# Score tiles of two head pairs in one row, sums over keys in place, and the products of a graph in a new order

## The chip, the cores and the metric

The kernel runs on one core of one Trainium2 chip. The metric is the device time in microseconds (us), lower being better. The engines that work here are TensorE (PE in the profile, its weight loads PEld), VectorE (DVE), ScalarE (ACT) and SyncE (SP), which issues all DMAs. GpSimd is idle.

## The reference

Two graph layers are applied one after the other to 32 graphs of 512 nodes with 512 features each, in float32. The first is attention with 8 heads of 64, weighted by the adjacency, with a residual and a layer norm; the second is a graph attention whose logits are a sum of two scalars per node pair. Cut to what matters:

```python
# layer 0
q, k, v = x @ Wq.T + bq, x @ Wk.T + bk, x @ Wv.T + bv      # per head: 512 x 64
logits  = q @ k.T / sqrt(64) + log(clip(adj, 1e-8))        # per head: 512 x 512
x1      = layer_norm(x + softmax(logits) @ v @ Wo.T + bo)
# layer 1
f       = x1 @ fc_w.T + fc_b
masked  = leaky((f @ q_w + q_b) + (f @ k_w + k_b).T + (1 - adj) * -1e9)
out     = softmax(masked) @ f + x1
```

## The kernel before

**Tiling.** A graph's matrices lie in SBUF as four chunks of 128 partitions. Heads are worked in pairs: two heads of 64 fill 128 partitions, so a graph has four *slots*, p = 0 to 3 (`slot(b, p)`, L1278). The attention is kept transposed, keys on partitions: for each of four key chunks kc, `score` (L838) multiplies kT by qT for both heads (two matmuls of 64 rows each, 512 columns, into two PSUM banks), and ScalarE writes exp of it into a tile `at` of 128x2x512 (L858; L856 where the tile is *halved*, that is, where its two halves lie in two single banks). `factors` (L861) multiplies by the clipped adjacency `cT` (L866), which gives the same weights as adding its logarithm before the exponential. `values` (L881, matmul L891) multiplies v by `at`, two heads side by side in columns of 64. `sums` (L871) adds the four `at` of a pair into a tile `as` (L876, L879), and `divide` (L902, matmul L908) sums `as` over the partitions with a matrix of ones, 32 columns at a time. The sums go to DRAM and back (`d0`, `c`), are inverted in `divided` (L922) and come back spread over all partitions as `R`, with which `scale` (L942) multiplies the values' results `oT`.

**Products in seven parts.** The products q and k (`seven_qk`, L624), v (`seven_v`), with Wo (`seven_wo`), Z = softmax x (`seven_z`, L1001) and the last with fc_w (`seven_out`, L779) are done on 2x2 blocks with seven half-size products each instead of eight, by additions on VectorE between them. They all go through `halves` (L210): 128 rows, 64 columns, two matmuls side by side. In `seven_z`, `before0`, `before1`, `after0`, `after1`, `before2`, `after2` and `after3` are these additions; product 6 needs what `after0` writes.

**PSUM.** The pool ps_s has two tiles of two banks each, which scores and the q/k products use in turn; ps_o has one bank for the values; `lone` is a list of three single banks mx, my, mz for the other products, for `divide` (the first of them) and for halved score tiles (the other two).

**Stages.** Three graphs are in work at once. While graph b is in its four slots, graph b-1 gets Wo, the norm and its layer 1 logits, and graph b-2 gets Z and the output. The weights of layer 1 of graph b-1 are made by `softmax` (L1117), a list of units from `weigh_units` (L424): logits of chunks 0 and 1, of 2 and 3, then `weights` (leaky on VectorE and exp on ScalarE by turns, L446 and L447), then `blocks`, which spreads the result e into the tile `eP` by 16 DMAs of 64 KB (L148). `eT` (L1074) transposes eP in blocks of 32 on VectorE (L572); Z of the graph cannot start before. The three users of the io pool's one buffer (x of the next graph, the work tile w, and eP) take turns.

**Order.** The order on TensorE, VectorE, ScalarE and SP is the order in which the program calls the operations; no planner changes it, and each engine takes its own list from front to back. In a slot the order is: first half of the last pair's values, score tiles 0 and 1, factors of them, score tiles 2 (halved) and 3, `divide` in slots 0 and 2, second half of the values, and then a product of that slot: Z in slot 0, Wo in slot 1, the output in slot 2 (`layer1_rows`, L1418), v of the next graph in slot 3. The q/k products of the next pair are laid between. The tag `at` has 6 buffers and `as` 2.

Of the kernel before, what the change touches and what calls it, by code (L numbers as in the profile page):

```python
# [19 lines left out]
P = 128  # L20
# [10 lines left out]
def kernel(  # L31
# [392 lines left out]
    def weigh_units(s, small, work, name):  # L424


        e = s["e"]
        s["r"] = small.tile([P, NC], FP, tag="r", name=f"r_{name}")
        top = small.tile([P, NC], FP, tag="top", name=f"top_{name}", bufs=2)
        nm = small.tile([P, NC], FP, tag="nm", name=f"nm_{name}", bufs=2)  # L430

        def logits(cs):
            for c in cs:
                qk = work[c % len(work)]
                nc.scalar.activation(qk, s["kb"], AF.Identity, bias=s["q"][:, c : c + 1])  # L435
# [27 lines left out]
    def scaled(s, cs):  # L463
        nc.vector.tensor_mul(s["yb"][:, cs, :], s["n"][:, cs, :], over(K["gamma"], cs))
# [39 lines left out]
    def fast(ctx):  # L504
# [333 lines left out]
        def score(b, p, kc, apart=False):  # L838

            s = S[b]  # L840
            halved = kc == 2 and not apart
            if halved:
                parts = lone[1:]
            else:
                sc = ps_s.tile([P, 2, N], FP, tag="s", name=f"sc_{b}_{p}_{kc}")
                parts = [sc[:, j, :] for j in range(2)]
            for j in range(2):
                rows = slice(j * DK, (j + 1) * DK)
                nc.tensor.matmul(  # L849
                    parts[j], s["kT", p][rows, ts(kc, P)], s["qT", p][rows, :],  # L850
                    start=True, stop=True,
                )
            at = act.tile([P, 2, N], FP, tag="at", name=f"at_{b}_{p}_{kc}", bufs=6)
            if halved:
                for j in range(2):
                    nc.scalar.activation(at[:, j, :], parts[j], AF.Exp, scale=SCALE)  # L856
            else:
                nc.scalar.activation(at, sc, AF.Exp, scale=SCALE)  # L858
            s["at", p, kc] = at
# [103 lines left out]
        def divide_here(b, p):  # L963

            s = S[b]
            ps = ps_s.tile([P, 2, N], FP, tag="s", name=f"ps_{b}_{p}")[:, 0, :]
            i = 2 * B - 1 + p % 2
            R = act.tile([P, 2, N], FP, tag="at", name=f"t_{b}_{p}", bufs=6)  # L970
# [146 lines left out]
        def softmax(b):  # L1117
            s = S[b]
            units = weigh_units(
                s, small, [s["w"][:, i, :] for i in ((2, 3, 0) if b == B - 1 else (2, 3))], b  # L1120
            )

            def blocks():
                s["eP"] = io.tile([P, NC, N], FP, tag="x", name=f"eP_{b}")
                spread_blocks(s["eP"], s["e"])
            return units + ([blocks] if b < B - 2 else [])

        def new_yb(b):
            S[b]["yb"] = act.tile([P, NC, D], FP, tag="yb", name=f"yb_{b}")

        def last_layer1(b):
# [5 lines left out]
            S[b]["yb"] = yb = K["qk_s"].rearrange("p a b f -> p (a b) f")[:, :NC, :]  # L1137
            places = []
            for i in range(6):
                t = act.tile([P, 2, N], FP, tag="at", name=f"l1_{i}", bufs=6)  # L1140
# [133 lines left out]
        def run(units):  # L1274
            for u in units:
                u()

        def slot(b, p):  # L1278
# [14 lines left out]
                wos[0]("a")  # L1293
            run(vals[:1])
            for kc in (0, 1):
                score(b, p, kc)
            if first:
                run(first_v[1:2])
            if p == 0 and last >= 0:
# [15 lines left out]
                if last >= 0:  # L1315
                    mask(S[last])
            for kc in (2, 3):
                score(b, p, kc, first)
            if p == 0 and last >= 0:
                divide(last, 2)  # L1320
            if p == 2 and b != 1:
                divide(b, 0)
            run(vals[1:])
            if p == 1 and last >= 0:
# [1 line left out]
            soft = softmax(last) if p == 3 and last >= 0 else []  # L1326
            run(soft[:1])
            if p == 0 and last >= 0:
                if b >= 2:
                    new_yb(b - 2)  # L1330
                    scaled(S[b - 2], slice(0, KH))
                    zs, extra = seven_z(b - 2)
                    extra[0]()
                    run(eT(b - 2))
                if b == 1:
                    turn_a((2, 3))
            if p > 0 or b < 2:
                factors(b, p, 1)
# [6 lines left out]
            if p == 0 and b >= 2:  # L1345
                extra[1]()
                run(next_qk[:4])
                zs[0]()
                extra[2]()
                run(next_qk[4:])  # L1350
                extra[3]()
                zs[1]()
                turn_a((2, 3))
                scaled(S[b - 2], slice(KH, NC))
                extra[4]()
                zs[2]()
                extra[5]()
                divided(last, 2)
                zs[3]()
                factors(b, p, 1)  # L1360
                extra[6]()
                sums(b, p, 0)
            elif p == 0:
# [54 lines left out]
        def layer1_rows(b, next_qk, norm):  # L1418
# [10 lines left out]
            run(norm[2:])  # L1429
            if b == 1:  # L1430
                run(next_qk[2:4])
                divide(b, 0)
            elif nxt == B:
                sums(b, 2, 0)
            if b >= 2 and nxt < B:
# [36 lines left out]
        def run_out(units):  # L1472
            for mul, add in units:
                mul()
                add()

        def last_slot(rest):


            b, last = B - 1, B - 2  # L1480
            for kc in (0, 1):
                score(b, 3, kc)
            run(values(b, 2))
            factors(b, 3, 0)
            sums(b, 3, 0)
# [1 line left out]
            soft = softmax(last)  # L1487
            soft[0]()
            for kc in (2, 3):
                score(b, 3, kc, True)  # L1490
            factors(b, 3, 1)
            load_e(b)
            vs = values(b, 3)
# [61 lines left out]
            outs[1][0]()  # L1555
            run(soft[:2])
            outs[2][0]()
            soft[2]()
            outs[3][0]()
            for i in range(1, 4):  # L1560
                outs[i][1]()
# [2 lines left out]
            return rest_of_layer1(find_range(), outs[4][1])  # L1564

        load_x(0)
        pair = act.tile([P, 2, N], FP, tag="at", name="first_pair", bufs=6)
        pair = [pair[:, i, :].rearrange("p (c d) -> p c d", c=DC) for i in range(2)]
        load_first_constants(pair)
        load_a(0, range(NC))  # L1570
# [167 lines left out]
```

## Time and profile before

| | |
|---|---|
| time, median of 3 runs | 3359.99 us (3356.05 to 3360.93) |
| profiled execution: its own time | 3363.72 us |
| its span, first to last instruction | 3361.9 us |
| TensorE busy, matmuls recorded | 3343.2 us (99%), 25914 |
| VectorE busy | 3004.2 us (89%), 5284 instructions |
| ScalarE busy | 1394.7 us (41%), 2501 instructions |
| DMA, share of 16 engines and mean rate | 36.2%, 75 GB/s |
| granted TensorE clock | 1.000 |

The busy table gives the time in which an engine had an instruction in work. Matmuls overlap, so a busy TensorE says little of its pace; the distance between the starts of its weight loads in the timeline says more. A timeline line has the start in us from the span's start, the time from there to the end of the group, the engine, the line of the kernel, the operation with its output and inputs, the mode and shape, how many instructions were merged (x), and in brackets the idle time ahead of it and what ended it. For a matmul, 128*64 means 128 rows by 64 columns of the array. Some matmul records are missing from a trace.

### The profile page before, as it was taken

How to read it: one execution, taken by the hardware profiler on the slowest of the kernel's cores; microseconds unless marked ns; L12 is line 12 of the kernel's file. 1: busy time of each engine (PE TensorE's matmuls, PEld its weight loads, DVE VectorE, ACT ScalarE, POOL GpSimd, SP SyncE). 2: the span in 40 equal slices, each digit the busy share in tenths (PEclk: the TensorE clock that was granted, in tenths of full speed). 3: DMA queues.
4: the chain of work that ended last, by engine and by line, in shares of the span. 5: the costliest groups of instructions: out<-in, count | busy, mean ns of one | idle time of the engine just before them, and what ended most of it. 6: DMA issues, size and time to landing. Idle time of an engine off the chain costs nothing.

```text
span 3361.9 us, 64316 instructions
## 1 busy us (share of the span) xinstructions
PE 3343.2 (99%) x25914; PEld 1886.9 (56%) x25914; DVE 3004.2 (89%) x5284; ACT 1394.7 (41%) x2501; POOL 0.9 (0%) x9
## 2 busy tenths in 40 slices
PE   9999999999999999999999999999999999999999
PEld 4555555555555555555555555555555555555555
DVE  7898989889998899898898988999889988889897
ACT  3443443434443444434444343443344443444443
POOL 0000000000000000000000000000000000000000
PEclk9999999999999999999999999999999999999999
DMA  4334333343423443333424334333344333443321
GB/s 126 50 69 92 63 87 70 58 92 79 74 71 59 88 91 62 80 67 70 92 61 88 68 61 92 68 85 67 58 92 85 68 76 65 76 91 62 84 72 45
DMA packets 881656, 252.85 MB, mean 75 GB/s; under 512 B 806732, under 2 KB 809036, under 8 KB 881352
## 3 DMA queue, kind: packets, MB, share of 16 engines
q1 hardware_dynamic: 881352, 248.67, 36.2%
q8 instruction: 206, 3.38, 0.4%
q14 instruction: 98, 0.80, 0.1%
HBM read 182.46 MB, written 34.65 MB: 65 GB/s over the span
## 4 chain that ended last, share of the span: by engine, by line
PE 94%; DVE 2%; SPq 2%; DMA 1%; ACT 1%; issue 0%; DVEq 0%; ACTq 0%
PE f L213 21%; PE my L213 15%; PE mx L213 14%; PE mz L213 14%; PE po L891 13%; PE sc L849 10%; SPq L148 1%; PE my L849 1%; PE mz L849 1%; PE mx L849 1%; DVE at L866 1%; PE my L908 1%; PE mx L908 1%; PE mz L908 1%; SPq L542 1%
## 5 line engine op out<-in xcount | busy, mean ns | idle before, releaser
L858 ACT ACTIVATE at<-sc 128x1024 f32<-128x1024 f32 x386 | 384.5, 1031 | 751.2 <-PE sc L849 751.2
L866 DVE SCALAR_TENSOR_TENSOR at<-cT,at 128x1024 f32<-128x1024 f32 x512 | 600.2, 1215 | 67.0 <-ACT at L858 67.0
L891 PE MATMUL po<-at,v 128*64 128x512 f32 x2048 | 490.0, 599 | 2.0 <-DVE fold_more L298 1.6
L849 PE MATMUL sc<-qT,kT 64*128 64x512 f32 x1544 | 387.6, 607 | 0.0
L879 DVE TENSOR_TENSOR as<-as,at 128x1024 f32<-128x1024 f32 x254 | 310.3, 1222 | 5.4
L891 PEld LDWEIGHTS po<-at,v 128*64 128x64 f32 x2048 | 135.8, 136 | 271.3 <-issue 248.6
L849 PEld LDWEIGHTS sc<-qT,kT 64*128 64x128 f32 x1544 | 138.3, 186 | 225.1 <-issue 171.9
L213 PE MATMUL f<-xT,wq 128*64 128x256 f32 x2032 | 262.6, 379 | 0.0
L213 PE MATMUL f<-T,qk_s 128*64 128x256 f32 x2032 | 251.7, 379 | 0.6 <-ACT f L651 0.6
L213 PEld LDWEIGHTS f<-xT,wq 128*64 128x64 f32 x2032 | 146.0, 137 | 100.6 <-issue 28.0
L213 PEld LDWEIGHTS f<-T,qk_s 128*64 128x64 f32 x2032 | 145.7, 137 | 74.6 <-ACT f L651 1.4
L876 DVE TENSOR_TENSOR as<-at,at 128x1024 f32<-128x1024 f32 x128 | 155.8, 1217 | 0.1
L657 ACT ACTIVATE qT<-f,bq 128x256 f32<-128x256 f32 x127 | 60.2, 474 | 229.6 <-PE f L213 229.6
L663 ACT ACTIVATE kT<-f,bk 128x256 f32<-128x256 f32 x127 | 59.8, 471 | 192.2 <-PE f L213 192.2
L213 PE MATMUL f<-xT,qk_s 128*64 128x256 f32 x1016 | 131.3, 379 | 0.0
L213 PE MATMUL f<-T,wk 128*64 128x256 f32 x1016 | 131.3, 379 | 0.0
L213 PE MATMUL f<-xT,wk 128*64 128x256 f32 x1016 | 131.3, 379 | 0.0
L213 PE MATMUL mz<-eP,n 128*64 128x256 f32 x960 | 114.3, 380 | 2.0 <-DMA c<-d 1.1
L213 PE MATMUL mx<-eP,n 128*64 128x256 f32 x960 | 114.2, 380 | 1.3 <-DVE eP L572 1.3
L213 PE MATMUL my<-eP,n 128*64 128x256 f32 x960 | 114.1, 379 | 0.5 <-DVE eP L572 0.5
L899 ACT COPY oT<-po 128x512 f32<-128x512 f32 x128 | 74.9, 585 | 71.9 <-PE po L891 71.9
L435 ACT ACTIVATE w<-w,q 128x512 f32<-128x512 f32 x128 | 85.3, 716 | 32.9 <-DVE top L436 24.9
(419 smaller groups left out, 6107.0 us busy)
## 6 DMA issues: line engine op xcount, KB each, us to landing
cT<-in_adj_dram SPq DMA_DIRECT2D x512, 64.0 KB
R<-d SPq DMA_DIRECT2D x126, 256.0 KB
x<-in_x_dram SPq DMA_DIRECT2D x124, 256.0 KB
n<-in_x_dram SPq DMA_DIRECT2D x31, 1024.0 KB
L<-in_adj_dram SPq DMA_DIRECT2D x60, 512.0 KB
eP<-L SPq DMA_DIRECT2D x480, 64.0 KB
out_dram<-yb SPq DMA_DIRECT2D x58, 512.0 KB
w<-dk SPq DMA_DIRECT2D x32, 256.0 KB
```

What stands on the lines that cost most here:

```text
L213: nc.tensor.matmul(to[ts(h, DK)], left[:, ts(h, DK)], right, start=start, stop=stop, skip_group_check=True,)
L435: nc.scalar.activation(qk, s["kb"], AF.Identity, bias=s["q"][:, c : c + 1])
L657: nc.scalar.activation(q[:, H:], ps["a"], AF.Identity, bias=bq)
L663: nc.scalar.activation(k[:, :H], ps["d"], AF.Identity, bias=bk, scale=-1.0)
L849: nc.tensor.matmul(parts[j], s["kT", p][rows, ts(kc, P)], s["qT", p][rows, :], start=True, stop=True,)
L858: nc.scalar.activation(at, sc, AF.Exp, scale=SCALE)
L866: nc.vector.scalar_tensor_tensor(at, cT[:, kc, :].unsqueeze(1).to_broadcast([P, 2, N]), ADJ_MIN, at, ALU.max, ALU.mult,)
L876: nc.vector.tensor_add(s["as", p], s["at", p, 0], s["at", p, 1])
L879: nc.vector.tensor_add(s["as", p], s["as", p], s["at", p, kc])
L891: nc.tensor.matmul(s["po", p][j * DK : (j + 1) * DK, :], s["v"][h // 4][:, kc, ts(h % 4, DK)], s["at", p, kc][:, j, :], start=(kc == 0), s ...
L899: nc.scalar.copy(s["oT"][p], s["po", p])
L908: nc.tensor.matmul(ps[h * BL : (h + 1) * BL, :], ones[:, :BL], s["as", p + h // 2][:, h % 2, :], start=True, stop=True,)
```

## The change

For graphs 2 to 30 the four slots become two halves, `first_two` (pairs 0 and 1) and `second_two` (pairs 2 and 3). Each half starts with the sum over keys of an earlier two pairs (`divide`), then makes all eight score tiles of its two pairs in a row (`eight_scores`; every third tile, counting from the first, is halved), and has all its products and both pairs' values (`both`) behind them. Between those the factors are applied one tile at a time (`factor`). The sums over keys are added into the pair's first attention tile after the values have read it (`sums_in_place`), so that no tile `as` is needed; `at` gets 8 buffers. In layer 1, leaky becomes a unit of its own, ahead of the four exponentials, and the logits use three parts of w instead of two for every graph. All 16 loads of cT for the next graph are issued together, after the last factor. The last graph's first slot becomes `joining_slot`, its other slots stay; graphs 0 and 1 keep the slots, with the part for b >= 2 taken out of `slot`.

```diff
@@ weigh_units @@
-        def weights():
+        def leaky():
             nc.vector.tensor_scalar_mul(nm, top, -LEAKY_SLOPE)
             nc.vector.scalar_tensor_tensor(nm, top, -1.0, nm, ALU.mult, ALU.min)
             for c in range(NC):
                 ec = e[:, c, :]
                 nc.vector.scalar_tensor_tensor(ec, ec, LEAKY_SLOPE, ec, ALU.mult, ALU.max)
+
+        def weights():
+            for c in range(NC):
+                ec = e[:, c, :]
                 nc.scalar.activation(
                     ec, ec, AF.Exp, bias=nm[:, c : c + 1], accum_out=s["r"][:, c : c + 1]
                 )
-        return [lambda: logits((0, 1)), lambda: logits((2, 3)), weights]
+        return [lambda: logits((0, 1)), lambda: logits((2, 3)), leaky, weights]
@@ score, sums @@
-            halved = kc == 2 and not apart
...
-            at = act.tile([P, 2, N], FP, tag="at", name=f"at_{b}_{p}_{kc}", bufs=6)
+            at = act.tile([P, 2, N], FP, tag="at", name=f"at_{b}_{p}_{kc}", bufs=8)
...
-                s["as", p] = act.tile([P, 2, N], FP, tag="as", name=f"as_{b}_{p}", bufs=2)
+                s["as", p] = act.tile([P, 2, N], FP, tag="at", name=f"as_{b}_{p}", bufs=8)
...
+        def factor(b, p, kc):
+            at = S[b]["at", p, kc]
+            nc.vector.scalar_tensor_tensor(
+                at, cT[:, kc, :].unsqueeze(1).to_broadcast([P, 2, N]), ADJ_MIN, at,
+                ALU.max, ALU.mult,
+            )
+        def both(b, p):
+            run(values(b, p))
+        def sums_in_place(b, p):
+            s = S[b]
+            to = s["as", p] = s["at", p, 0]
+            return [
+                lambda kc=kc: nc.vector.tensor_add(to, to, s["at", p, kc]) for kc in range(1, NC)
+            ]
@@ softmax @@
-                s, small, [s["w"][:, i, :] for i in ((2, 3, 0) if b == B - 1 else (2, 3))], b
+                s, small, [s["w"][:, i, :] for i in (2, 3, 0)], b
@@ new functions @@
+        def eight_scores(b, ps):
+            n = 0
+            for p in ps:
+                for kc in range(NC):
+                    score(b, p, kc, n % 3 == 0)
+                    n += 1
+        def first_two(b):
+            last, nxt = b - 1, b + 1
+            if b == 2:
+                run(values(last, 3))
+                run(seven_qk(b, 1))
+                scale(last, 0)
+            divide(last, 2)
+            eight_scores(b, (0, 1))
+            new_yb(b - 2)
+            scaled(S[b - 2], slice(0, KH))
+            zs, extra = seven_z(b - 2)
+            extra[0]()
+            run(eT(b - 2))
+            extra[1]()
+            extra[3]()
+            factor(b, 0, 0)
+            zs[0]()
+            extra[2]()
+            factor(b, 0, 1)
+            scaled(S[b - 2], slice(KH, NC))
+            turn_a((2, 3))
+            zs[1]()
+            extra[4]()
+            factor(b, 0, 2)
+            zs[2]()
+            extra[5]()
+            divided(last, 2)
+            factor(b, 0, 3)
+            zs[3]()
+            extra[6]()
+            load_n(last)
+            load_x(nxt)
...
+            first_difference(last, third)
+            wos, wo_adds = seven_wo(last, long_banks(last))
+            wos[0]()
+            both(b, 0)
+            next_qk = seven_qk(b, 2)
+            next_qk[0]()
+            both(b, 1)
+            run(sums_in_place(b, 0))
+            scale(last, 2)
+            first_sum(last)
+            run(next_qk[1:4])
+            run(sums_in_place(b, 1))
...
+        def joining_slot(b):
+            last = b - 1
+            divide(last, 2)
+            for kc in range(NC):
+                score(b, 0, kc, kc == 0)
...
+            zs[0]()
+            extra[2]()
+            factor(b, 0, 0)
...
+        def second_two(b):
+            last, nxt = b - 1, b + 1
+            divide(b, 0)
+            eight_scores(b, (2, 3))
+            z_sums(b - 2)
+            ks, qs = dots_units(S[last], small, S[b]["R", 0][:, 1, :], last)
+            run(xT(nxt))
+            differences(nxt)
+            norm = normalise_units(S[last], small, last)
+            factor(b, 2, 0)
+            muls, adds = seven_out(b - 2)
+            muls[0]()
+            adds[0][0]()
+            norm[0]()
+            run(norm[1:])
+            factor(b, 2, 1)
...
+            factor(b, 2, 3)
+            muls[2]()
+            run(ks)
+            store_k(S[last], small, dram, last)
+            load_k(S[last], work(last)[:, 1, :])
...
+            factor(b, 3, 3)
+            load_a(nxt, range(NC))
+            both(b, 2)
+            next_qk = seven_qk(nxt, 0)
+            run(next_qk[:2])
+            both(b, 3)
+            run(qs)
+            mask(S[last])
+            run(next_qk[2:4])
+            soft = softmax(last)
+            soft[0]()
+            soft[1]()
+            run(next_qk[4:])
+            soft[2]()
+            divided(b, 0)
+            vs = seven_v(nxt)
+            vs[0]()
+            vs[1]()
+            soft[3]()
+            soft[4]()
+            run(sums_in_place(b, 2))
+            vs[2]()
+            run(sums_in_place(b, 3))
+            vs[3]()
+            scale(b, 0)
+            turn_a((0, 1))
+            run(seven_qk(nxt, 1))
@@ loop over graphs @@
-            for p in range(NPAIR):
+            if 2 <= b < B - 1:
+                first_two(b)
+                second_two(b)
+                continue
+            if b == B - 1:
+                joining_slot(b)
+            for p in range(b == B - 1, NPAIR):
```

More of the change, by code (lines that the diff above doesn't have):

```diff
@@ L836, in other_banks, with score @@
             return tiles
-        def score(b, p, kc, apart=False):
+        def score(b, p, kc, halved):
             s = S[b]
-            halved = kc == 2 and not apart
             if halved:
@@ L969, in divide_here @@
             i = 2 * B - 1 + p % 2
-            R = act.tile([P, 2, N], FP, tag="at", name=f"t_{b}_{p}", bufs=6)
+            R = act.tile([P, 2, N], FP, tag="at", name=f"t_{b}_{p}", bufs=8)
             t, r = R[:, 0, :], R[:, 1, :]
@@ L1139, in last_layer1 @@
             for i in range(6):
-                t = act.tile([P, 2, N], FP, tag="at", name=f"l1_{i}", bufs=6)
+                t = act.tile([P, 2, N], FP, tag="at", name=f"l1_{i}", bufs=8)
                 places += [t[:, j, :].rearrange("p (c n) -> p c n", c=KH) for j in range(2)]
@@ L1295, in slot @@
             for kc in (0, 1):
-                score(b, p, kc)
+                score(b, p, kc, False)
             if first:
@@ L1317, in slot @@
             for kc in (2, 3):
-                score(b, p, kc, first)
+                score(b, p, kc, kc == 2 and not first)
             if p == 0 and last >= 0:
                 divide(last, 2)
-            if p == 2 and b != 1:
+            if p == 2:
                 divide(b, 0)
@@ L1328, in slot @@
             if p == 0 and last >= 0:
[L1329 to L1338, printed above, removed]
+                turn_a((2, 3))
+            factors(b, p, 1)
             if p == 3 and last >= 0:
@@ L1344, in slot @@
                 next_qk = seven_qk(nxt, 0)
[L1345 to L1363, printed above, removed]
+            if p == 0:
                 sums(b, p, 0)
@@ L1431, in layer1_rows @@
                 run(next_qk[2:4])
-                divide(b, 0)
             elif nxt == B:
@@ L1475, in run_out @@
                 add()
+        def eight_scores(b, ps):
[24 more added lines that the diff above has]
+            scaled(S[b - 2], slice(KH, NC))
+            turn_a((2, 3))
+            zs[1]()
[9 more added lines that the diff above has]
+            load_x(nxt)
+            factor(b, 1, 0)
+            factor(b, 1, 1)
+            factor(b, 1, 2)
+            factor(b, 1, 3)
+            first_difference(last, third)
[11 more added lines that the diff above has]
+            run(next_qk[4:])
+            next_qk = seven_qk(b, 3)
+            wos[1]()
+            offset_rows(S[b - 2], slice(0, KH))
+            run(wo_adds[0])
+            wos[2]()
+            wo_adds[1][0]()
+            offset_rows(S[b - 2], slice(KH, NC))
+            run(wo_adds[1][1:])
+            wos[3]()
+            run(wo_adds[2])
+            next_qk[0]()
+            wos[4]()
+            run(wo_adds[3])
+            run(next_qk[1:4])
+            run(stats_units(S[last], small, last))
+            invert(S[b - 2])
+            run(next_qk[4:])
@@ new lines, in joining_slot @@
+        def joining_slot(b):
[3 more added lines that the diff above has]
+                score(b, 0, kc, kc == 0)
+            new_yb(b - 2)
+            scaled(S[b - 2], slice(0, KH))
+            zs, extra = seven_z(b - 2)
+            extra[0]()
+            run(eT(b - 2))
+            extra[1]()
+            extra[3]()
+            zs[0]()
+            extra[2]()
+            factor(b, 0, 0)
+            scaled(S[b - 2], slice(KH, NC))
+            turn_a((2, 3))
+            zs[1]()
+            extra[4]()
+            factor(b, 0, 1)
+            zs[2]()
+            extra[5]()
+            divided(last, 2)
+            factor(b, 0, 2)
+            zs[3]()
+            extra[6]()
+            factor(b, 0, 3)
+            first_difference(last)
+            sums(b, 0, 0)
@@ new lines, in second_two @@
+        def second_two(b):
[14 more added lines that the diff above has]
+            factor(b, 2, 1)
+            adds[0][1]()
+            muls[1]()
+            adds[1][0]()
+            factor(b, 2, 2)
+            adds[1][1]()
+            adds[1][2]()
+            load_e(last, 0)
+            factor(b, 2, 3)
[3 more added lines that the diff above has]
+            load_k(S[last], work(last)[:, 1, :])
+            run(adds[2])
+            muls[3]()
+            load_e(last, 1)
+            run(adds[3])
+            factor(b, 3, 0)
+            factor(b, 3, 1)
+            factor(b, 3, 2)
+            factor(b, 3, 3)
[10 more added lines that the diff above has]
+            soft[1]()
+            run(next_qk[4:])
+            soft[2]()
[12 more added lines that the diff above has]
+            run(seven_qk(nxt, 1))
@@ L1481, in last_slot @@
             for kc in (0, 1):
-                score(b, 3, kc)
+                score(b, 3, kc, False)
             run(values(b, 2))
@@ L1489, in last_slot @@
             for kc in (2, 3):
-                score(b, 3, kc, True)
+                score(b, 3, kc, False)
             factors(b, 3, 1)
@@ L1557, in last_slot @@
             outs[2][0]()
-            soft[2]()
+            run(soft[2:])
             outs[3][0]()
@@ L1566, in fast @@
         load_x(0)
-        pair = act.tile([P, 2, N], FP, tag="at", name="first_pair", bufs=6)
+        pair = act.tile([P, 2, N], FP, tag="at", name="first_pair", bufs=8)
         pair = [pair[:, i, :].rearrange("p (c d) -> p c d", c=DC) for i in range(2)]
```

## The prediction, made before the changed kernel ran

> **What bounds the kernel now.** I read the page's busy table and chain first, then one period (the work between two score blocks of the same slot, one graph per period) in the timeline, engine by engine.
>
> ```profile
> PE 3343.2 (99%) x25914; PEld 1886.9 (56%) x25914; DVE 3004.2 (89%) x5284; ACT 1394.7 (41%) x2501; POOL 0.9 (0%) x9
> PE 94%; DVE 2%; SPq 2%; DMA 1%; ACT 1%; issue 0%; DVEq 0%; ACTq 0%
> ```
>
> TensorE is the bound, and VectorE, at 89%, is close behind it. The weight loads (PEld) of the timeline show TensorE's pace better than its busy time, for matmuls overlap:
>
> ```profile
> 1507.86 0.14 PEld L891 LDWEIGHTS po<-at,v 128*64 128x64 f32 x2 [0.28 <-issue]
> 1508.82 0.30 PEld L849 LDWEIGHTS sc<-qT,kT 64*128 64x128 f32 x4 [0.81 <-PE po L891]
> 1509.35 0.19 PEld L849 LDWEIGHTS sc<-qT,kT 64*128 64x128 f32 x2 [0.24 <-issue]
> ...
> 1511.50 0.19 PEld L849 LDWEIGHTS sc<-qT,kT 64*128 64x128 f32 x2 [0.24 <-issue]
> 1512.45 0.20 PEld L891 LDWEIGHTS po<-at,v 128*64 128x64 f32 x4 [0.76 <-issue]
> 1512.93 0.14 PEld L891 LDWEIGHTS po<-at,v 128*64 128x64 f32 x2 [0.29 <-issue]
> ```
>
> A step of 512 columns takes 0.43 us, 16 loads of the 256-column products 1.727. From 1507.86 the third step should load at 1507.86+1.29=1509.15; it does at 1509.35: going from 128*64 to 64*128 costs **0.20**. Going back, 1511.50+1.29=1512.79 against 1512.93: **0.14**. With the sums over keys (128*32) between scores and values, 1536.85 to 1539.28 holds five steps (2.15) and 0.28 more, so each of its two turns costs 0.14. Score blocks start at 1508.82 and 1612.20: a period of **103.38 us**. It holds four blocks, two of them with a sum: 4x0.20+2x0.14+2x0.28=1.64 of turns. Another 0.11 is a short wait in the Z products. All else is gapless.
>
> **The Trainium skill.** "TensorEngine Tiling (Array Packing)", section Key Properties: changing the tiling mode drains TensorE. The trace agrees (0.14 to 0.20 each). "ScalarE: Activation LUTs", section What ACT_TABLE_LOAD costs: 186 ns + 0.833 ns per element, about 93 ns of it overlapped. For 1024 that is 1039; the row of L858 has 1031, and two exponentials in a row start 0.915 apart. "DMA: Bandwidth & Descriptors", section Anatomy of one DMA: about 2.0 us fixed, mostly the write receipt. Here:
>
> ```profile
> 1324.30 11.62 SPq L148 DMA_DIRECT2D eP<-L  x16
> ...
> 1337.92 0.71 DVE L572 STREAM_TRANSPOSE eP<-eP 128x512 f32<-128x512 f32 x1 [1.35 <-DMA d<-R]
> ```
>
> The 16 issues end at 1335.92; VectorE, idle, gets eP at 1337.92. That is 2.0 after the last issue, and it decides below.
>
> **The change, part by part** (29 periods, b=2 to 30).
>
> *Turns.* Two blocks of eight score tiles per graph, each reached through the sum over keys: per block 0.14 (128*64 to 128*32) + 0.20 + 0.14 back = 0.48, so 0.96 per graph against 1.64: **-0.68**. The second 0.20 is assumed (32 to 64*128 does not occur in this trace); at 0.28 the gain would be 0.52, at 0.14 0.80. The number of matmuls does not change.
>
> *Eight tiles in a row.* TensorE makes a tile in 0.86; ScalarE takes 0.915 for a whole and 0.95 for a halved one:
>
> ```profile
> 1509.99 1.94 ACT L858 ACTIVATE at<-sc 128x1024 f32<-128x1024 f32 x2 [12.57 <-PE sc L849]
> 1511.82 0.60 ACT L856 ACTIVATE at<-mx 128x512 f32<-128x512 f32 x1
> 1512.29 0.62 ACT L856 ACTIVATE at<-my 128x512 f32<-128x512 f32 x1
> 1512.77 1.06 ACT L858 ACTIVATE at<-sc 128x1024 f32<-128x1024 f32 x1
> ```
>
> Three tiles fit (two of ps_s, one in two lone banks). Tile n needs the banks of n-3. The first exponential starts 1.50 after the block's nominal start X (1508.49 here, from the third step). Tile 3 loads at X+2.58 and its banks come free at 2.58; by tile 7 it is X+6.02 against 6.31. The load runs 0.24 ahead of need, so about **+0.07** per block (0 to 0.5, if ScalarE starts late; the sum's copy in front of it is over 0.4 before).
>
> *VectorE's new order.* The same work (about 93.5 us a period), but all products wait for long runs of it. In the second half, counting from the first load of the out-products: VectorE stands still until ScalarE has done the copy of product 1 and Ln, Exp (1.73+0.43+0.52+0.59=3.27). Then it runs without rest: norm 0.86, factor 1.135, two adds 0.78, subtraction 0.61, factor 1.13, two adds 0.78 end at 8.57; product 7, due at 8.64, needs them 0.2 before its load: +0.10. On with two adds, factor 1.13, ks 3.55, eight adds 3.1, four factors 4.54 to 21.85; the last value product of pair 3 is due at 21.44 and has 0.24 slack: +0.17. Then qs 3.07, mask 1.37, logits 2.46, adds 1.0, leaky 2.7, divided 0.6, six sums 7.3, three v adds 1.8, scale 1.2, turn 1.2, q/k adds 1.1. These free the bank of the next block's second score tile at 45.6. The second v-unit ends at 32.2 and that tile loads 13.05 later, at 45.25: late, but by little more than the 0.24 slack, +0.1 at most, and this lies inside the Z wait below. With 0.07 for this block they make **+0.34** (0 to 1.2: a run of 41 us without rest is known to some half us).
>
> *The spread of e into eP.* Formerly it was issued with two slots' work to go (1530.83) and used at 1544.49, after scores, values and the next q/k products. Now the four exponentials of the weights stand on ScalarE behind the second v-unit's copies. From the end v1 of that unit: 0.43 to the copy, 0.49, four at 0.705 (2.82), 0.1: SP starts at v1+3.84. (SP's other path, divided(b,0) and its two R loads of 1.31, ends about then: it hides; at 2.04, as in some periods, it adds 0.6.) Sixteen issues take 10.77 at least in this trace, up to 12.13; with 2.0 eP lands at v1+16.6 to 17.2. From there eT 2.52, before1 1.21, after1 0.60, factor 1.135, after0 0.61+0.69, 0.11 to TensorE = 6.88: product 6 of Z can load at v1+23.5 to 24.1. TensorE gets there at v1+5.18 (v2, v3)+6.04 (q/k)-0.21 (shift of loads, 256 to 512 columns)+1.20 (sum and turns)+7.23 (block)+3.45 (products 1, 5)=22.89, and 23.0 with the old 0.11. So **+0.5 to +1.0**, taken as +0.75; 0 if issue is quicker, 1.8 with late R loads and slow issues. What is queued behind eT on VectorE (factors of pair 0, second scaled, turn_a) all precedes the values, which start 12 us later, so it recovers.
>
> *The joining slot* (b=31) has only four tiles ahead of Z, 3.44 less cover, and no factor before after0: about **+3** once: eP lands 4.7 after the block's start and product 6 loads 5.74 later, at 10.4 instead of 7.25.
>
> *At nothing:* sums in place replace one add into as and two in place by three in place (same 1.22 each; they wait for the values, read 3 us before); eight at tiles free up before the next block (values and sums of the last are done; the sum over keys stands ahead of it); the third w buffer and leaky apart only remove alternation ScalarE has room for (41%); d0, c, d1, R loads, x and n loads keep 5 us or more; cT, now 16 issues after the last factor (about 8.5 us), is used 20 us on; the adjacency half for the mask is issued 7 us ahead, where the last took about 4.3 to land (the burst ends near 1511.5 after the issue at 1507.21): cover 2.5 us, then VectorE would wait.
>
> *Sum:* -0.68+0.34+0.75=+0.41; x29=+12; with the joining slot **+15**. The profiled execution took 3363.7 (span 3361.9); the median of the runs shown is 3360.0, to which I add it: **3375**.
>
> **The rivals.** *eP in time (0.26):* if the 16 issues take under 10.2 us, as their median of 0.63 each would allow, or land sooner, the Z wait falls away. It decides at eP landing by X+3.75 after the next block's start. Then -0.68+0.1 to 0.34: 3343 to 3350. For it: the old issues came just behind 8 cT loads, the new do not. Against: no issue in the periods I read took under 10.77. *VectorE becomes the bound (0.15):* the 41 us run is late by 1 us or more, at values and the second tile: +1 to 1.5 per period, 3390 to 3405. *ScalarE paces the blocks (0.11):* copies ahead of the first exponential hold it back and each block costs 0.5: 58x0.5=29 more than the turns give back: 3385 to 3395. That the change does not regroup at all is excluded: the order is written out by hand.
>
> **How the numbers follow.** The likeliest case (0.48) spans 3362 to 3390. A measurement of this kernel tells 0.2%, 6.7 us, from no change; of this case 0.13 lies within that. Faster 0.24 (from eP in time), same 0.15 (0.02 from there), slower 0.61. The range 3343 to 3402 takes in the first rival and most of the second.
>
> **What would show it.** Right: 64*128 loads in two blocks a graph; a wait of 1 to 3 us on VectorE ahead of the transposes of eP in nearly every period (now 6 of 30), and a gap of TensorE in front of Z's product 6 of 0.5 to 1; the period 103.6 to 104.2. Wrong: no eP wait and a period of 102.8 to 103 (first rival); TensorE waiting at values or at the second score tile for VectorE (second); ScalarE releasing score loads with gaps (third).

## The result: 24 us slower, and the profile after

The changed kernel takes **3384.77 us** (median of 4 runs, 3383.92 to 3386.41) against 3360.46 for the kernel before, run beside it (3356.05 to 3361.81): a ratio of 1.0075, 95% interval 1.0058 to 1.0093. The profiled execution took 3383.92, its span is 3382.1, 20.2 us longer than before; the granted clock is 1.0. The forecast was 3375, slower.

First the busy table and the chain of work that ended last, of the changed kernel:

```profile
PE 3332.2 (99%) x25914; PEld 2032.1 (60%) x25914; DVE 3001.1 (89%) x5313; ACT 1408.8 (42%) x2559; POOL 0.9 (0%) x9
PE 79%; DVE 13%; ACT 3%; DMA 2%; SPq 2%; issue 1%; DVEq 0%; ACTq 0%
```

The busy shares say nothing: TensorE still has 99%, with the same number of matmuls. The chain tells it. TensorE's share of it fell from 94% to 79%, and VectorE's rose from 2% to 13%, ScalarE's and the transfers' with it: somewhere TensorE now waits for VectorE, which waits for a transfer.

Where, the timeline shows. This is TensorE's loads around a block of eight tiles (start and length in us):

```profile
1547.25 0.79 PEld L213 LDWEIGHTS f<-xT,wk 128*64 128x64 f32 x8
1548.42 0.16 PEld L930 LDWEIGHTS mz<-at,ones 128*32 128x32 f32 x8 [0.39 <-DVE oT L968]
...
1549.95 0.19 PEld L852 LDWEIGHTS sc<-qT,kT 64*128 64x128 f32 x2 [0.24 <-issue]
...
1556.50 1.49 PEld L213 LDWEIGHTS mz<-eP,n 128*64 128x64 f32 x16 [0.76 <-DVE eP L576]
1558.07 1.65 PEld L213 LDWEIGHTS mx<-R,third 128*64 128x64 f32 x16
1561.31 1.52 PEld L213 LDWEIGHTS mz<-eP,n 128*64 128x64 f32 x16 [1.59 <-ACT L L1053]
1562.88 1.68 PEld L213 LDWEIGHTS my<-eP,n 128*64 128x64 f32 x16
```

Products follow each other by 1.727. From product 5 of Z (1558.07) to product 2 (1562.88) should be two of these, 3.45; it is 4.81. The extra 1.36 stands in front of product 6, at 1561.31. The bracket names ScalarE's copy at L1053, but that had ended at 1560.82. What product 6 needed last is VectorE's second subtraction of `after0`, which ends at 1561.19. Everything ahead of it in that chain, back to SP, is late:

```profile
1541.01 10.77 SPq L148 DMA_DIRECT2D eP<-L  x16
```

```profile
1554.43 2.49 DVE L576 STREAM_TRANSPOSE eP<-eP 128x512 f32<-128x512 f32 x4 [2.47 <-DMA eP<-L]
...
1558.77 1.22 DVE L887 SCALAR_TENSOR_TENSOR at<-cT,at 128x1024 f32<-128x1024 f32 x1
1559.91 0.69 DVE L1077 TENSOR_TENSOR eP<-eP,R 128x512 f32<-128x512 f32 x1
1560.51 0.68 DVE L1078 TENSOR_TENSOR n<-third,n 128x512 f32<-128x512 f32 x1
```

VectorE stood still for 2.47 us, and from then on it has work without a gap up to `after0`. The list of VectorE's waits (total, number, longest) shows that this is the rule; the second line is the kernel before:

```profile
DVE eP L576 <- DMA d<-R: 61.9, 26, 3.4
```

```profile
DVE eP L572 <- DMA d<-R: 8.3, 6, 1.9
```

61.9 us in 26 waits; the other four periods are listed with "DMA eP<-L" as releaser. (d<-R is SP's next transfer behind the 16 of eP; the instruction that waits, the transpose of eP, is the one to trust.) All 30 periods have this wait, where six had it before. For graphs 3 to 30 the gap in front of product 6 is 0.6 to 1.8; in six of these 28 product 5 comes late too, by 0.2 to 1.0, for it reads what `before1` makes of the transposed eP.

The distance from one sum over keys (L930, before L908) to the next gives a ledger by halves. Before, a half takes 51.69, in 22 of the 29 periods in both of them; single halves of the others have up to 53.37, which makes a mean period of 103.63. Now second halves take 51.46 with hardly an exception, first halves 51.84 to 54.04, in the mean 52.81 (of graphs 3 to 30; that of graph 2, the first of its kind, is left out of what is said of first halves: it takes 51.84 to 51.85 even where no eP is late). The sum over keys at the start of graph 2 and that at the start of graph 31, 29 periods on, are 3023.5 us apart, before 3005.2: **+18.3**. The two ends together, where work was only exchanged between the last slot of graph 1 and the first half of graph 2 and where the joining slot is, make +1.9.

### The profile page after: what moved, and what is told of

It is laid out like the page before. It is cut to its first block, busy times and chain, and to the rows that moved or that the text cites. A ratio compares the mean times of both kernels' runs of the same rounds, so it can differ in the third digit from the quotient of the medians.

```text
span 3382.1 us, 64140 instructions
## 1 busy us (share of the span) xinstructions
PE 3332.2 (99%) x25914; PEld 2032.1 (60%) x25914; DVE 3001.1 (89%) x5313; ACT 1408.8 (42%) x2559; POOL 0.9 (0%) x9
## 4 chain that ended last, share of the span: by engine, by line
PE 79%; DVE 13%; ACT 3%; DMA 2%; SPq 2%; issue 1%; DVEq 0%; ACTq 0%
PE f L213 20%; PE my L213 12%; PE mx L213 12%; PE mz L213 12%; PE po L913 11%; PE sc L852 5%; DVE at L887 3%; SPq L148 2%; DVE eP L576 2%; PE my L852 1%; DVE R L392 1%; DVE yb L801 1%; DMA d<-R 1%; PE mz L852 1%; PE mx L852 1%
## 5 line engine op out<-in xcount | busy, mean ns | idle before, releaser
L887 DVE SCALAR_TENSOR_TENSOR at<-cT,at 128x1024 f32<-128x1024 f32 x468 | 553.9, 1214 | 0.0
L913 PE MATMUL po<-at,v 128*64 128x512 f32 x2048 | 468.7, 594 | 2.0 <-DVE fold_more L298 1.6
L900 DVE TENSOR_TENSOR at<-at,at 128x1024 f32<-128x1024 f32 x348 | 423.8, 1218 | 8.0
L861 ACT ACTIVATE at<-sc 128x1024 f32<-128x1024 f32 x328 | 332.0, 1070 | 53.4 <-PE sc L852 53.4
L852 PE MATMUL sc<-qT,kT 64*128 64x512 f32 x1312 | 317.3, 593 | 0.4 <-ACT at L861 0.4
L913 PEld LDWEIGHTS po<-at,v 128*64 128x64 f32 x2048 | 156.5, 137 | 237.2 <-issue 154.2
L852 PEld LDWEIGHTS sc<-qT,kT 64*128 64x128 f32 x1312 | 120.1, 186 | 165.7 <-ACT at L861 79.8
L655 ACT COPY f<-f 128x256 f32<-128x256 f32 x127 | 45.3, 357 | 345.3 <-PE f L213 345.3
L576 DVE STREAM_TRANSPOSE eP<-eP 128x512 f32<-128x512 f32 x120 | 74.7, 680 | 72.4 <-DMA d<-R 61.9
L852 PE MATMUL my<-qT,kT 64*128 64x512 f32 x254 | 133.5, 605 | 0.0
L852 PE MATMUL mz<-qT,kT 64*128 64x512 f32 x248 | 130.5, 606 | 0.0
L213 PE MATMUL mz<-eP,n 128*64 128x256 f32 x960 | 116.0, 381 | 11.3 <-DVE n L1078 11.3
```

The lines of the kernel that those rows point to most:

```text
L213: nc.tensor.matmul(to[ts(h, DK)], left[:, ts(h, DK)], right, start=start, stop=stop, skip_group_check=True,)
L576: lambda c=c: nc.vector.transpose(dst[:, c, :], src[:, c, :]) for c in range(4)
L655: nc.scalar.copy(ps["b"], ps["a"])
L852: nc.tensor.matmul(parts[j], s["kT", p][rows, ts(kc, P)], s["qT", p][rows, :], start=True, stop=True,)
L887: nc.vector.scalar_tensor_tensor(at, cT[:, kc, :].unsqueeze(1).to_broadcast([P, 2, N]), ADJ_MIN, at, ALU.max, ALU.mult,)
L900: lambda kc=kc: nc.vector.tensor_add(to, to, s["at", p, kc]) for kc in range(1, NC)
```

## The experiments

"After" is the changed kernel, 3384.8 us; each comparison with the kernel before was made on the chip of the run. Three theories were to be told apart: *late eP* (TensorE waits because the spread of e lands too late), *VectorE is the bound*, and *ScalarE paces the score blocks*.

**1. VectorE's order behind eP** (`first_two`).

```diff
             extra[1]()
-            extra[3]()
-            factor(b, 0, 0)
             zs[0]()
             extra[2]()
+            extra[3]()
+            factor(b, 0, 0)
             factor(b, 0, 1)
```

> Only the order of VectorE's work after the transposes of eP is changed: after0 comes before after1 and the factor of pair 0, chunk 0, so product 6 of Z needs eP 1.74 us less early (0.60 for after1, 1.14 for the factor). Theory (late eP): the time lost per period is TensorE's wait in front of product 6, about 1.35 us in the mean (first halves of 52.80 us against 51.4 without a wait); nearly all of it goes, a rest of 0.1 to 0.2 stays where product 5 waits in the latest periods. 29 x 1.2 = 35: about 3350 us, below both kernels. Rival (VectorE is the bound): the same work in another order, 3385 +- 4. Rival (ScalarE paces the score blocks): 3385 +- 4.

Measured: 3375.52 us, ratio to the kernel before 1.0044 (1.0031 to 1.0058). That is 9 us less than after, not 35: a miss for all the theories as they stood. TensorE's loads:

```profile
1556.68 1.65 PEld L213 LDWEIGHTS mx<-R,third 128*64 128x64 f32 x16
1558.52 1.54 PEld L213 LDWEIGHTS mz<-eP,n 128*64 128x64 f32 x16 [0.19 <-issue]
1560.13 1.65 PEld L213 LDWEIGHTS my<-eP,n 128*64 128x64 f32 x16
1561.86 1.65 PEld L213 LDWEIGHTS mz<-eP,n 128*64 128x64 f32 x16
1564.26 1.49 PEld L213 LDWEIGHTS mx<-eP,n 128*64 128x64 f32 x16 [0.74 <-DVE n L1084]
1566.60 1.49 PEld L213 LDWEIGHTS mz<-eP,n 128*64 128x64 f32 x16 [0.84 <-DVE L L1088]
```

The wait in front of product 6 is down to 0.1, as expected. But product 3 (1564.26) now waits for `before2`, and product 4 (1566.60) for `after2`. VectorE's lines between say why:

```profile
1557.11 0.69 DVE L1077 TENSOR_TENSOR eP<-eP,R 128x512 f32<-128x512 f32 x1 [0.46 <-PE mz L213]
...
1561.20 1.22 DVE L468 TENSOR_TENSOR yb<-n,gamma 128x1024 f32<-128x1024 f32 x1
1562.33 1.30 DVE L598 STREAM_TRANSPOSE cT<-cT 128x512 f32<-128x512 f32 x2
1563.55 0.65 DVE L1084 TENSOR_TENSOR n<-n 128x512 f32<-128x512 f32 x1
```

`after0` overwrites a quarter of eP that product 1 reads, so it can't start before 1557.11, when that product is through. From there VectorE works without a gap, and the second `scaled` (L468) and the turn of cT stand ahead of `before2`. Nearly every first half took 52.47 to 52.48, wherever eP landed: 1.11 over the 51.36 that later runs showed without waits. So what is paid here in nearly every period is no longer the landing but the length of VectorE's own list: `after1` and the first factor, which had stood ahead of `after0`, now stand between it and `before2`, and the next products in line meet the delay.

**2. The weights later** (`second_two`): exponentials and spread go behind the third v unit.

```diff
-            soft[3]()
-            soft[4]()
             run(sums_in_place(b, 2))
             vs[2]()
+            soft[3]()
+            soft[4]()
```

> The four exponentials of the weights and the 16 transfers of eP are put behind the third v unit (ScalarE's copy of product 4), so eP starts about 1.8 us later. Theory (late eP): every one of these microseconds is paid, 29 x 1.8 = +52: about 3437 us. Rival (VectorE is the bound): eP is not what sets the end, 3385 to 3392. Rival (ScalarE paces the blocks): 3385 to 3392.

Measured: 3424.6 us, ratio 1.0190 (1.0175 to 1.0206), 40 more than after. One period in the trace, SP's issues and TensorE's load of product 6:

```profile
1558.87 12.07 SPq L148 DMA_DIRECT2D eP<-L  x16
```

```profile
1579.82 1.52 PEld L213 LDWEIGHTS mz<-eP,n 128*64 128x64 f32 x16 [2.02 <-ACT L L1053]
```

The transposes of eP start in the mean 7.44 after the sum over keys, against 6.05: later by 1.39 rather than 1.8. First halves became longer by 54.19-52.81=1.38, and 29x1.38=40. Each microsecond of landing is paid in full, and the other two theories, which had no change, fall. The size was off because here SP starts right after the last exponential in all 29 periods, while in after the R loads had already held it up in 12 of them.

**3. Less work for VectorE**: the sums over keys of graphs 2 to 30 without their fourth chunk.

```diff
-                lambda kc=kc: nc.vector.tensor_add(to, to, s["at", p, kc]) for kc in range(1, NC)
+                lambda kc=kc: nc.vector.tensor_add(to, to, s["at", p, kc]) for kc in range(1, NC - 1)
```

> The fourth key chunk is left out of the sums over keys of graphs 2 to 30: one add of 128x1024 less per pair, four of 1.22 us, 4.9 us per graph less for VectorE. Theory (late eP): VectorE's total is not what binds, and these adds lie neither between the transposes of eP and product 6 nor ahead of the exponentials: 3385, at most 5 less. Rival (VectorE is the bound): the 1.35 us per period come back whole, 29 x 1.35 = 39 less: about 3346 us. Rival (ScalarE paces the blocks): 3385.

Measured: 3384.09 us (3383.24 to 3385.91): no change. VectorE's busy time falls from 3001.1 to 2876.7 us, 4.3 per graph, and that brings nothing, since these adds don't lie between what is late and who waits.

**4. eP through two queues.**

```diff
-                nc.sync.dma_start(
+                (nc.sync, nc.gpsimd)[j % 2].dma_start(
```

> Half of the 16 transfers of eP are issued by GpSimd, which is idle, the other half by SP, so that the last issue comes about 5.5 us earlier (if GpSimd issues at SP's rate; up to 2 us less if it is slower by half). Nothing else changes. Theory (late eP): eP lands before it is needed, the wait on VectorE and that in front of product 6 go: 3384.8 - 29 x 1.35 = 3346 us, and 3342 if the wait of 0.11 that was there before goes as well. Rival (VectorE is the bound): 3385 +- 4. Rival (ScalarE paces the blocks): 3385 +- 4.

Measured: **3342.89 us** (3342.24 to 3345.83), ratio 0.9949 (0.9935 to 0.9963): 42 less than after and 18 less than before. First halves are 51.36 nearly throughout, and the chain of work is TensorE's again:

```profile
PE 96%; DVE 2%; ACT 1%; DMA 0%; issue 0%; SPq 0%; DVEq 0%; ACTq 0%
```

The way there differs from the expectation. The two queues in one period:

```profile
1523.37 5.13 POOL L148 DMA_DIRECT2D eP<-L  x8 [97.69 <-PE mx L213]
```

```profile
1523.09 9.18 SPq L148 DMA_DIRECT2D eP<-L  x8
```

SP's eight issues took 9.18, where all 16 had taken 10.77. So the last issue came not 5.5 earlier but 2.0 (mean 1.87 after the sum over keys, against 3.91). It was enough: in the mean the transposes start 4.01 after that sum in place of 6.05, which is 2.04 earlier, and first halves had exceeded 51.36 by 1.45.

**5. The kernel before, with two queues**: the same edit in the kernel before.

> The kernel before with half of eP's 16 transfers issued by GpSimd and nothing else. Theory: it loses only the waits of its own 6 late periods, 0.26 per period in the mean (103.64 against 103.38): 29 x 0.26 = 7.5 less, about 3353 us; what lies between this and the changed kernel with two queues (3342.9) is then the gain of the regrouping itself, turns less new waits, 0.34 x 29 = 10. Rival (GpSimd's issues help for a reason other than eP's landing, such as SP's other transfers): the gain is that of the changed kernel, 40 us: 3320.

Measured: 3354.94 us (3353.36 to 3357.39), ratio 0.9982 (0.9975 to 0.9989), 6.3 less. All its halves are 51.69 to 51.70. So the kernel before lost 6 to 7 us to the same cause, and what lies between this run and the fourth experiment, **11 to 12 us** (the lower figure from the two ratios, since the runs were made on two chips), is what the regrouping is worth when eP is in time. That both kernels gain in step with their own late halves, 6 us here and 42 there, speaks against the rival, which gave 3320.

**6. Filling VectorE's wait** (one queue, `first_two`).

```diff
             scaled(S[b - 2], slice(0, KH))
+            scaled(S[b - 2], slice(KH, NC))
             zs, extra = seven_z(b - 2)
             extra[0]()
+            factor(b, 0, 0)
             run(eT(b - 2))
             extra[1]()
-            extra[3]()
-            factor(b, 0, 0)
             zs[0]()
             extra[2]()
+            extra[3]()
             factor(b, 0, 1)
-            scaled(S[b - 2], slice(KH, NC))
             turn_a((2, 3))
```

> SP's 16 issues and eP's landing stay as they are. VectorE's order in the first half: the second scaled and the factor of pair 0, chunk 0, go ahead of the transposes of eP, into VectorE's own wait for eP (2.3 us, they take 2.27), and after0 comes ahead of after1. So product 6 needs eP earlier by nothing more than 1.74 us of VectorE's work in between, as in the first experiment, but before2 comes 2.27 us sooner after eP than there, so product 3 should not wait any more. Theory (late eP: a late tile delays VectorE's whole queue, and each next product meets it until the queue has caught up): 29 x (1.4 - 0.15) = 36 less than the changed kernel: about 3348 us. Rival (what is taken from product 6's wait comes back behind it whatever the order is, because VectorE has no room in this half): 3370 to 3378, as the first experiment.

Measured: **3344.71 us** (3341.39 to 3346.16), ratio 0.9951 (0.9937 to 0.9964). The theory of late eP, mended by the first experiment, gave 3348; the rival, 3370 to 3378, falls. VectorE's lines, then TensorE's:

```profile
1535.13 2.34 DVE L468 TENSOR_TENSOR yb<-n,gamma 128x1024 f32<-128x1024 f32 x2
...
1537.98 1.22 DVE L887 SCALAR_TENSOR_TENSOR at<-cT,at 128x1024 f32<-128x1024 f32 x1
1539.95 2.49 DVE L576 STREAM_TRANSPOSE eP<-eP 128x512 f32<-128x512 f32 x4 [0.75 <-DMA c<-d]
```

```profile
1543.28 1.52 PEld L213 LDWEIGHTS mx<-R,third 128*64 128x64 f32 x16 [0.32 <-ACT at L861]
1545.09 1.52 PEld L213 LDWEIGHTS mz<-eP,n 128*64 128x64 f32 x16 [0.29 <-issue]
1546.66 1.68 PEld L213 LDWEIGHTS my<-eP,n 128*64 128x64 f32 x16
```

The transposes start as late as ever (6.13 after the sum over keys in the mean), but the wait holds work that formerly came behind it; in this period 0.75 of it is left. First halves are 51.36 with a few up to 51.92.

**7. No halved tiles in the blocks of eight**, on top of two queues.

```diff
-                    score(b, p, kc, n % 3 == 0)
+                    score(b, p, kc, False)
```

> On top of the kernel with two queues for eP (3342.9): no halved tiles in the blocks of eight, so only the two tiles of ps_s take turns. This shows what a block paced by ScalarE looks like. Theory (with a third tile in the lone banks ScalarE's eviction costs 0.02 to 0.07 per block): each of the last six tiles must now wait for the eviction of the tile two before it, 0.35 to 0.5 us per tile, 2 to 3 per block, 58 blocks: 3460 to 3517 us. Rival (the halved tiles make no difference; the blocks are paced by ScalarE with them too): 3343 to 3350.

Measured: 3442.25 us in one run. Both halves became longer by much the same, 53.05 against 51.46 and 53.21 against 51.36: 1.6 to 1.85 per block, 0.3 per tile for the last six, somewhat under what was expected. The waits of the score loads for ScalarE in after and in this run (total, number, longest):

```profile
PEld sc L852 <- ACT at L861: 79.8, 184, 1.2
```

```profile
PEld sc L852 <- ACT at L861: 294.2, 358, 1.6
```

This is what a block paced by ScalarE looks like. The first line, 79.8 us, is the largest named wait of TensorE's loads in after, and yet not lost time: loads run ahead of the matmuls, and from the block's nominal start (1549.09, two steps of 0.43 ahead of 1549.95 above) to that of product 1 (1556.34, one product ahead of 1558.07) are 7.25 us; eight tiles of 0.86, the turn of 0.14 and the shift of loads of 0.21 make 7.23.

**8. Both remedies and one more move**: experiments 4 and 6 together, and in `second_two`:

```diff
-            factor(b, 2, 2)
             adds[1][1]()
             adds[1][2]()
+            factor(b, 2, 2)
```

> Two queues for eP, VectorE's order of the sixth experiment, and in the second half the factor of pair 2, chunk 2, behind the two adds that free the banks for product 7 of the output. Theory: what is left over the kernel with two queues (3342.9) is the wait of 0.08 in front of product 7 and single late periods: 2 to 4 us, 3340. Rival (VectorE has no room left, a factor put back makes the values wait instead): 3343 to 3346.

Measured: 3361.34 us (3360.6 to 3362.76), ratio 1.0001 (0.9993 to 1.0009): 17 to 18 slower than either remedy alone, and outside both expectations. The rival named the mechanism, values that wait for a factor put back, but put its cost far too low. First halves are 51.36 throughout; second halves rose from 51.46 to 52.15, and 29x0.69=20. The wait that the move should remove had cost nothing. In after, the loads of product 2, 7 and 4 of the output:

```profile
1511.79 1.66 PEld L213 LDWEIGHTS my<-fc,L 128*64 128x64 f32 x16
1513.60 1.57 PEld L213 LDWEIGHTS mx<-fc,third 128*64 128x64 f32 x16 [0.15 <-DVE yb L801]
1515.24 1.65 PEld L213 LDWEIGHTS mz<-fc_s,L 128*64 128x64 f32 x16
```

The middle one is 0.08 late, but from the first to the third it is 3.45, two products at full pace: the load was late, the matmuls were not. The move itself made VectorE wait for TensorE:

```profile
1502.07 0.68 DVE L795 TENSOR_TENSOR L<-L 128x512 f32<-128x512 f32 x1
1503.35 0.88 DVE L801 SCALAR_TENSOR_TENSOR yb<-mx,r,yb 128x256 f32<-128x256 f32 x2 [0.60 <-PE mx L213]
```

and these 0.60 were paid at the values of pair 3, which then took VectorE's pace of one factor, 1.13, per key chunk:

```profile
1514.12 0.79 PEld L213 LDWEIGHTS f<-xT,wq 128*64 128x64 f32 x8
1515.16 0.23 PEld L913 LDWEIGHTS po<-at,v 128*64 128x64 f32 x4 [0.25 <-issue]
1516.23 0.20 PEld L913 LDWEIGHTS po<-at,v 128*64 128x64 f32 x4 [0.84 <-DVE at L887]
1517.37 0.20 PEld L913 LDWEIGHTS po<-at,v 128*64 128x64 f32 x4 [0.94 <-DVE at L887]
1518.50 0.20 PEld L913 LDWEIGHTS po<-at,v 128*64 128x64 f32 x4 [0.94 <-DVE at L887]
1518.99 0.14 PEld L213 LDWEIGHTS f<-T,wk 128*64 128x64 f32 x2 [0.29 <-issue]
```

From the q/k product ahead of the values (1514.12) to the one behind them (1518.99) are 4.87 us. In after the same two loads are 4.19 apart:

```profile
1522.99 0.79 PEld L213 LDWEIGHTS f<-xT,wq 128*64 128x64 f32 x8
...
1527.18 0.14 PEld L213 LDWEIGHTS f<-T,wk 128*64 128x64 f32 x2 [0.28 <-issue]
```

Without a wait it would be 4.08 (0.86, and 3.22 as at the values of pair 2). The second half is where VectorE has no room: the rival "VectorE becomes the bound" has its place here, and the changed kernel stays just short of it.

## Why the prediction was right in its direction, and where its size came from

**Direction and mechanism: right.** The likeliest case was that the spread of e comes too late and TensorE waits at Z's product 6 in every period. The trace shows the wait on VectorE in all 30 periods (1.45 to 3.42 us) and the gap at that product; experiments 2, 4 and 6 show that the landing of eP, and what stands behind it on VectorE, is the cause. The time, 3384.8, lies within the forecast's range and within its likeliest case; the period, 104.26, just above the 103.6 to 104.2 named as its sign.

**Turns, -0.68 per period: right.** From 1547.25 to 1549.95 runs the way 128*64 to 128*32 to 64*128, with the price assumed for the second turn (0.20), and the third step lies within 0.01 of where these prices put it.

**New waits apart from eP, +0.34: too high, +0.12.** With eP in time the halves are 51.36 and 51.46, a period of 102.82 against 103.38: -0.56, that is -0.68 and +0.12. Product 7's 0.10 came as a late load and cost nothing. So did the "short wait in the Z products" of 0.11 before: there product 5 loads at 1548.12, product 6 late at 1549.96, but product 2 at 1551.57, two products on at full pace. ScalarE's 0.07 per block was 0.01 to 0.02. The values of pair 3 were late by 0.11 and paid it (0.17 foreseen).

**eP, +0.75: the term that was mis-sized, by nearly half; +1.45** (52.81-51.36). No step was missing, but each was taken at or near its better end. From v1 on: start of SP's issues 3.84 foreseen, 4.16 in the mean, as the R loads, which "end about then", end later in 12 of 29 periods and then hold SP up; the 16 issues 10.77, the lowest figure, where the mean is 11.28, and was already 11.3 in the profile before; landing 2.0 after the last, which is 2.0 in most periods but up to 3.1 in single ones, 2.14 in the mean. In the mean eP came at v1+17.58, not 16.6 to 17.2. The chain behind it, 6.88 to product 6, and TensorE's arrival there held exactly.

**The base: an error the other way.** The sum was made against a period of 103.38, but the profiled execution before had a mean of 103.63, for it held seven late halves of its own; experiment 5 took them away, 6.3 us. The new wait takes their place, it doesn't come on top, so 7 us were to be taken off.

**The joining slot, about +3: right.** Product 2 of Z loads 12.61 us after the slot's sum over keys. In a first half without waits it is 13.10, less 3.44 for four tiles 9.66: +2.95. With two queues 1.14 of it is left (50.56 us from this sum over keys to the next become 48.74); there the transposes start without a wait, as soon as VectorE has done what stands ahead of them.

Together, against the profiled execution before: 29x(-0.68+0.12+1.45)=+25.8, less 7.2 for the base (3005.2-29x103.38), is 18.6, where the trace has 18.3 between the two sums over keys; the ends make it 20.2. The medians are 24.3 apart since the profiled execution before took 3.3 more than its median and that of the changed kernel 0.9 less. So it is in part luck that the forecast was only 10 us off: eP cost 20 us more than forecast, the new waits and the base took 13 to 14 back.

**The rivals.** *eP in time* gave 3343 to 3350, and with eP in time the kernel takes 3343 to 3345: its number was right, its condition was not met. What spoke for it, that the issues no longer stand behind loads of cT, made no difference (11.28 in the mean against 11.3). That VectorE's own order could give the time that was lacking was not in the prediction. *VectorE becomes the bound* did not happen, but by little (experiment 8). *ScalarE paces the blocks* did not.

**One reason was incomplete:** that what is queued behind eT "recovers" because it all precedes the values. It also precedes `before2` and `after2`, wanted by products 3 and 4, as experiment 1 showed. In the changed kernel it did recover: TensorE is late as well, and in the period shown VectorE waits 0.37 for TensorE ahead of `before2`, at 1565.05.

**A size at "nothing"** was off without harm: the 16 loads of cT take SP 12.99 us from 1523.87 in the period shown, not about 8.5. They end at 1536.86, before the next transfer of SP is wanted (1537.83).

## What to carry to other kernels

When the order of work is changed to save small costs on the bounding engine, follow each chain that crosses the engines (here ScalarE, SP, the transfers, VectorE) from its last input to its use, take the means and not the best of its steps, and see which idle time of before it had lived on. Where an engine waits for a late input, first look for work behind the wait that doesn't need it; drawing one consumer forward alone moved most of the wait to the next ones here. And a load marked as waiting is a loss only if the work after it comes later than at full pace: measure two products on.

## What the runs showed of the hardware that was not expected

The sixteen issues of eP from SP took 10.77 to 12.07 us in after, 0.67 to 0.75 each. With half of them given to GpSimd, whose eight took 5.13 to 5.27, SP's eight took 7.79 to 10.03, 0.97 to 1.25 each (6.74 to 8.66 in the kernel before with two queues, 0.84 to 1.08 each). So the time of an issue from SP is not a fixed price: it was longer when GpSimd issued at the same time. Something that both queues share may hold these transfers of 64 KB in 128-byte pieces back; that was not tested.
